# Causal attention: the next batch's part between values and scores, GpSimd's differences behind the parts, pauses around a transpose

## The chip, the cores and the metric

The kernel runs on one core of a Trainium2 chip. The metric is the device time of one execution in microseconds (us). TensorE (PE) multiplies matrices and transposes; its weight loads are shown as PEld. VectorE (DVE), ScalarE (ACT) and GpSimd (POOL) work on rows of 128 partitions; SyncE (SP) issues most transfers. Matrix products land in PSUM, of which the kernel uses eight banks, each 512 float32 wide, through one pool.

## The reference, cut to what matters

A network of four layers, each an attention and a mixture of experts, over 4 batches of 512 tokens of width 128, all in float32. Two of the four attentions are causal softmax attentions with 16 heads of width 8 for the values, and only these two run through the code that the change touches:

```python
# layer 0: scores with a bias by distance      # layer 1: scores as a product of two factors
att = einsum('bhtd,bhsd->bhts', q, k) / sqrt(D) + bias     logits = A1 * A2 * SCALE
att = softmax(where(causal, -inf, att))                    attn = softmax(where(causal, -inf, logits))
out = einsum('bhts,bhsd->bhtd', att, v) @ proj_w.T + b     out = einsum(attn, v) @ Wo.T + bo
```

Ahead of each attention a batch is normalized over its width (mean 0, variance 1). Layer 0's attention is followed by a top-1 routed mixture of experts whose routing is computed for each batch as soon as that batch's attention has ended.

## The kernel before, in words

**Units and steps.** `attention` (L566) works on 16 units: 4 batches b times 4 groups g of four heads. A unit has 4 steps j, one for each 128 queries; step j looks at the first (j+1)*128 keys. The work is a pipeline over units: while unit u is turned into weights and values, unit u+1 gets its scores. A step of the causal branch (L812 to L822) issues, in this order:

1. `weights(u, j)`: TensorE transposes the finished scores of unit u (1, 2, 4 and 4 PSUM banks for j = 0 to 3); ScalarE moves them to SBUF, with the exponential for two of the four heads.
2. `exponentials()`: ScalarE's exponentials for the other two heads of the scores made one step ago, kept in the list `put_off`.
3. `values_up_to`: TensorE multiplies the weights of the step before with the values.
4. `scores(u+1, j)`: four TensorE products into four banks; four DVE reductions (L604, L608) add bias or mask, find the largest of each row and write the scores `sc` to SBUF, which frees the banks; for two heads GpSimd then subtracts the largest (L605), right in this place of its queue.
5. the first slot, called "between" below (L821): one part of the next batch's beginning (`begin_next(u, True)`, not in units with u % 4 of 2 or 3), or else one part of a finished batch's routing (`go_on`).
6. at j = 0 `start(u+2)`, which forms the next unit's q and k (in layer 1 one product on DVE and one on GpSimd).
7. the second slot, called "tail" (L836 to L839): again a part of the next batch's beginning (not with u % 4 = 2), else of a routing.
8. on odd j a part of other work (`beside`: in layer 1 GpSimd's small copies and SP's loads of a later layer's weights), and at j = 2 and 3 the normalization and gathering of the unit before.

PE, DVE, ACT and POOL keep this order of the program in this region (`manual_schedule`); the queue of SP is put in order by a planner that uses its own costs. Where work of a later stage is placed among the attention's, that is the planner's too.

**The beginning of a batch** (`begin`, L968 for layer 0 and L1137 for layer 1) is a generator: each `yield` ends one part. Layer 0: (1) read and add the expert result; (2) statistics of tiles 0 and 1; (3) statistics of tiles 2 and 3 and GpSimd's reciprocal root (L157, L158); (4) DVE applies the norm to tiles 0 and 1 (L171); (5) to tiles 2 and 3; (6) `turned`: four TensorE transposes T (L180) into one bank and one copy nT by DVE or ACT (L127, L129, in turn); (7) q and k (L901 to L905); (8) values and the bias row (L857, L960). Layer 1 has no part (1), and its seventh place is three TensorE products "factors" (L1148), their copies, and nine transfers that write them to DRAM (L1155, L1159). Each unit of layer 1 later fetches its q and k factors from there with four transfers (L1176), issued three units ahead. Batch 0's parts all run ahead of the loop. For b = 1 the parts begin in unit 0; for b = 2 and 3 the first four run in the tails of units 3 and 7, and the rest in the slots of units 4 and 8.

**Routing** (`tokens`, L283) of a finished batch of layer 0 is a like generator of some 17 parts, from unit 4b+5 on, with its own norm, transposes, small products and, at its end, GpSimd's indirect transfers.

Of the kernel before, what the change touches and what calls it, by code (L numbers as in the profile page):

```python
# [11 lines left out]
AF = mybir.ActivationFunctionType  # L12
ALU = mybir.AluOpType
# [28 lines left out]
def kernel(ctx: ExitStack, tc: tile.TileContext, a: dict, out: bass.AP):  # L42
    nc = tc.nc
# [12 lines left out]
    def bank(name):  # L56
        return psum.tile([P, 512], FP, name=name, tag="bank", bufs=8)
# [66 lines left out]
    def copy(dst, src):  # L124
        n_copies[0] += 1
        if n_copies[0] % 2:
            nc.vector.tensor_copy(dst, src)  # L127
        else:
            nc.scalar.copy(dst, src)  # L129
# [46 lines left out]
    def transposed(src, tag):  # L176

        ps = bank(f"T_{tag}")
        for t in range(NT):
            nc.tensor.transpose(ps[:, t * P : (t + 1) * P], src[:, t, :], ident)  # L180
        return ps
# [6 lines left out]

    def turned(n, tag):

        nT = work.tile([P, S], FP, name=f"nT_{tag}", tag="nT", bufs=4)
        copy(nT, transposed(n, tag))
        yield
        return nT

# [370 lines left out]
    def attention(pool, tag, begin, project, residual, owT, added, after=None, beside=(), fetch=None):  # L566
# [8 lines left out]
        def begun(b):  # L575
            if ("begin", b) not in st:
                st["begin", b] = begin(b)
            return next(st["begin", b], "end") != "end"

        def start(u):  # L580
            b, g = units[u]
            if g == 0:
                st["o", b] = pool.tile([P, NT, NG, NG * HD], FP, name=f"otok_{tag}{b}", tag="otok")
            st["qk", u] = project(b, g)

        def product(ps, q, k, r, i, n0, n1):
            nc.tensor.matmul(  # L587
                ps[:, n0:n1], q[r : r + SLOT, i * P : (i + 1) * P], k[r : r + SLOT, n0:n1], start=True, stop=True
            )


        def scores(u, i):
            b, g = units[u]
            q, k = st["qk", u]
            n = (i + 1) * P
            banks = [bank(f"s_{tag}{u}_{i}{r}") for r in range(4)]
            for r in range(4):
                product(banks[r], q, k, r * SLOT, i, 0, n)
            for r in (2, 0, 3, 1):
                sc = pool.tile([P, n], FP, name=f"sc_{tag}{u}_{i}{r}", tag=f"sc{i}", bufs=4)  # L600
                top = small.tile([P, 1], FP, name=f"top_{tag}{u}_{i}{r}", tag="top", bufs=16)
                more = added(g * 4 + r)[:, S - n :]
                if r < 2:
                    nc.vector.tensor_tensor_reduce(sc, banks[r][:, :n], more, 1.0, -HUGE, ALU.add, ALU.max, top)  # L604
                    nc.gpsimd.tensor_scalar(sc, sc, top, None, ALU.subtract)  # L605
                else:

                    nc.vector.tensor_tensor_reduce(sc, banks[r][:, :n], more, -1.0, HUGE, ALU.add, ALU.min, top)  # L608
                    put_off.append((sc, top))
                st["sc", u, i, r] = sc  # L610

        put_off = []

        def exponentials():

            for sc, top in put_off:
                nc.scalar.activation(sc, sc, AF.Exp, bias=top, scale=-1.0)  # L617
            put_off.clear()

        def weights(u, i):  # L620
# [22 lines left out]
        def values_up_to(u, i):  # L643

            b, g = units[u]
            if i == 0:
                st["acc", u] = bank(f"acc_{tag}{u}")
            for j in range(i + 1):
                for r in range(4):
                    nc.tensor.matmul(  # L650
                        st["acc", u][r * SLOT : (r + 1) * SLOT, i * P : (i + 1) * P],
                        vpads[b % 2][:, j, g * 4 + r, :],
                        st["w", u, i, r][:, j * P : (j + 1) * P],
                        start=(j == 0),
                        stop=(j == i),
                    )
            if i == NT - 1:
                summed(u)
# [15 lines left out]
        def lowered(u):  # L674
            q, k = st["qk", u]
            ps = bank(f"low_{tag}{u}")
            for i in range(NT):
                nc.tensor.transpose(ps[:, i * P : (i + 1) * P], st["low", u][:, i, :], ident)  # L678
            ql = pool.tile([P, S], FP, name=f"ql_{tag}{u}", tag="ql", bufs=2)
            nc.vector.tensor_tensor(ql, ps, q, ALU.add)  # L680
            st["ql", u] = ql
# [20 lines left out]
        def together(*parts):  # L702

            live = [p for p in parts if p is not None]
            while live:
                for p in list(live):
                    made = next(p, None)
                    if made is None:
                        live.remove(p)
                    else:  # L710
                        made()
# [20 lines left out]
        def summed(u):  # L732
            o_u = pool.tile([P, S], FP, name=f"ou_{tag}{u}", tag="ou", bufs=3)
            nc.scalar.copy(o_u, st["acc", u])
            st["ou", u] = o_u
# [21 lines left out]
        rest = []  # L757
# [9 lines left out]
        def go_on():  # L767
            if rest and next(rest[0], "end") == "end":
                rest.pop(0)

        def begin_next(u, between=False):


            b = (u + 1) // NG + 1
            return u % NG not in ((2, 3) if between else (2,)) and b < NB and begun(b)
# [11 lines left out]
        with tc.manual_schedule(engines={E_.PE, E_.DVE, E_.Activation, E_.Pool}):  # L787
            while begun(0):
                pass
            for u in range(3):  # L790
                if fetch is not None:
                    fetch(*units[u])
                if u > 0:
                    start(u - 1)
            if added:
                for i in range(NT):
                    scores(0, i)
                    exponentials()
            else:

                for n in range(0, lead, 2):
                    if n == 2 * NT:
                        lowered(0)
                    together(step(largest, n), step(largest, n + 1))
            for u in range(n_units + 1):
                last = u - 1
                now, nxt = u < n_units, u + 1 < n_units
                for j in range(NT):
                    n = 2 * (u * NT + j)

                    of = (u, j - 1) if j > 0 and now else (last, NT - 1) if j == 0 and last >= 0 else None
                    if added:  # L812
                        if now:
                            weights(u, j)
                        exponentials()

                        if of:
                            values_up_to(*of)
                        if nxt:
                            scores(u + 1, j)  # L820
                        if rest or not begin_next(u, True):  # L821
                            go_on()  # L822
                    else:
                        together(step(largest, n + lead), step(by_key, n))
                        if of:
                            times_values(*of, 0)
                        if j == NT - 1 and nxt:
                            lowered(u + 1)
                        if rest or not begin_next(u, True):
                            go_on()  # L830
                        together(step(largest, n + 1 + lead), step(by_key, n + 1))
                        if of:
                            times_values(*of, 1)
                    if j == 0 and u + 2 < n_units:
                        start(u + 2)
                    if j == 0 and last >= 1 and units[last - 1][1] == NG - 1:  # L836
                        ended(units[last - 1][0])
                    elif not begin_next(u):
                        go_on()  # L839
                    if j % 2:  # L840
                        next(beside, None)
                    if j == 2 and last >= 0:
                        normalized(last)
                    if j == 3 and fetch is not None and u + 3 < n_units:
                        fetch(*units[u + 3])
                    if j == 3 and last >= 0 and units[last][1] == NG - 1:
                        gathered(units[last][0])
            ended(NB - 1)
            while rest:
                go_on()  # L850
# [275 lines left out]
    def l1_attn(beside):  # L1126
        with tc.tile_pool(name="attn1", bufs=2) as pool:
# [9 lines left out]
            def begin(b):  # L1137
                n = yield from normed(b, f"a1_{b}")
                nT = yield from turned(n, f"a1_{b}")


# [420 lines left out]
```

## Time and profile before

| | |
|---|---|
| median of 3 runs | 1575.8 us (1572.78 to 1575.96) |
| the profiled execution's own time | 1557.3 us |
| its span, first to last instruction | 1555.6 us |
| PE busy | 1279.9 us, 82% of the span |
| DVE, ACT, POOL busy | 866.6, 713.2, 657.2 us |
| mean granted TensorE clock | 0.898 |
| causal attention of layer 0 | from about 130 to 361 us |
| causal attention of layer 1 | from about 545 to 771 us |

Times inside the profile are microseconds from the start of the span. A line of the timeline gives start, duration, engine, line of the kernel, operation, what it writes and reads, shapes, how many like instructions are merged in it, and in brackets how long the engine had stood idle before it and what ended that. The list of waits gives, for an engine and a line, who released it, the sum in us, the number of times, and the longest. The profile is one execution; the runs of the first row are others.

### The profile page before, as it was taken

To read this page: it belongs to the slowest core of one execution; us is meant where nothing else is said; L and a number is where in the kernel's file an instruction comes from. 1 tells how busy PE (TensorE), PEld (TensorE's weight loads), DVE (VectorE), ACT (ScalarE), POOL (GpSimd) and SP (SyncE) were. 2 spreads that over 40 slices of the span, in tenths; PEclk is the share of its full clock that TensorE was granted. 3 is DMA by queue.
4 is the path that set the end of the run, shared out by engine and by line. 5 is a ranking of instruction groups with operands and counts; after the bars stand their busy time and mean duration, and the time that the engine had idled before them with its cause. 6 is when DMAs were issued, how large, how long until landed. Compare 5 with 4: busy or idle time off the path is not lost. (4 is left out here: it accounts for less than half of the span.)

```text
span 1555.6 us, 28883 instructions
## 1 busy us (share of the span) xinstructions
PE 1279.9 (82%) x10651; PEld 823.0 (53%) x10651; DVE 866.6 (56%) x2955; ACT 713.2 (46%) x1487; POOL 657.2 (42%) x791
## 2 busy tenths in 40 slices
PE   3787998995969688989989887819789999998394
PEld 3464666773755455757656666606533334333273
DVE  5325776773335366666556556615367787773343
ACT  1234876871443156768743322203336655564041
POOL 3455767772420177677510111263631224212253
PEclk9897999996989988999989878858979999999597
DMA  7520230002415375442022000014204000000233
GB/s 226 129 57 13 77 146 32 9 6 65 140 49 111 94 219 150 140 133 70 2 56 55 1 0 1 10 61 103 62 21 172 15 5 12 13 3 15 76 79 105
DMA packets 100660, 106.21 MB, mean 68 GB/s; under 512 B 9084, under 2 KB 73832, under 8 KB 100520
## 3 DMA queue, kind: packets, MB, share of 16 engines
q1 hardware_dynamic: 93864, 91.16, 20.8%
q0 software_dynamic: 6656, 13.22, 2.6%
q8 instruction: 84, 1.38, 0.4%
q14 instruction: 56, 0.46, 0.1%
HBM read 62.49 MB, written 41.85 MB: 67 GB/s over the span
## 5 line engine op out<-in xcount | busy, mean ns | idle before, releaser
L605 POOL TENSOR_SCALAR sc_a<-sc_a,top_a 128x128 f32<-128x128 f32 (+3 forms) x256 | 276.0, 1093 | 110.6 <-DVE top_a L604 75.1
L587 PE MATMUL s_a<-k_a,q_a 32*128 32x512 f32 (+3 forms) x1536 | 266.5, 548 | 17.1 <-POOL k_a L1183 13.8
L692 ACT ACTIVATE w_a<-t_a 128x512 f32<-128x512 f32 x256 | 140.4, 595 | 119.6 <-PE t_a L587 94.9
L628 PE MATMUL t_a<-ident,sc_a 128*128 128x128 f32 x1280 | 172.3, 282 | 6.2 <-DVE top_a L608 5.7
L489 POOL DMA_INDIRECT res_f<-y_f,back_f x112 | 109.8, 980 | 143.7 <-ACT y_f L488 102.3
L587 PE MATMUL t_a<-ql_a,k_a 32*128 32x512 f32 x512 | 168.8, 644 | 0.5 <-DVE low_a__12755 L672 0.2
L628 PEld LDWEIGHTS t_a<-ident,sc_a 128*128 128x128 f32 x1280 | 145.2, 144 | 36.4 <-issue 13.7
L617 ACT ACTIVATE sc_a<-sc_a,top_a 128x128 f32<-128x128 f32 (+3 forms) x256 | 134.9, 577 | 22.8 <-DVE top_a L608 22.6
L587 PEld LDWEIGHTS s_a<-k_a,q_a 32*128 32x128 f32 x1536 | 93.7, 188 | 88.1 <-issue 42.8
L637 ACT ACTIVATE w_a<-t_a 128x256 f32<-128x256 f32 (+2 forms) x192 | 94.3, 526 | 63.6 <-PE t_a L628 63.1
L395 POOL DMA_INDIRECT disp_f<-n_f,to_f x96 | 94.6, 985 | 66.7 <-issue 58.8
L501 PE MATMUL o_f<-w_l,h_f 128*128 128x128 f32 (+1 forms) x896 | 113.0, 279 | 3.8 <-DVE o_f L483 3.3
L501 PEld LDWEIGHTS o_f<-w_l,h_f 128*128 128x128 f32 (+1 forms) x896 | 103.0, 184 | 14.7 <-DVE o_f L483 6.0
L466 PE MATMUL h_f<-dT_f,w_l 128*128 128x320 f32 (+1 forms) x256 | 108.0, 560 | 2.8 <-ACT dT_f L444 2.8
L157 POOL TENSOR_SCALAR rs_f<-mv_f 128x4 f32<-128x4 f32 (+1 forms) x23 | 5.7, 248 | 230.0 <-DVE mv_f L154 229.2
L650 PE MATMUL acc_a<-w_a,vpad 128*32 128x128 f32 x2560 | 98.4, 280 | 0.6 <-DVE top_a L604 0.6
L639 ACT COPY w_a<-t_a 128x256 f32<-128x256 f32 (+2 forms) x192 | 93.7, 527 | 6.9 <-PE t_a L628 6.6
L672 DVE TENSOR_REDUCE low_a__12755<-s_a 128x1 f32<-128x512 f32 x128 | 82.1, 685 | 26.3 <-PE t_a L587 18.5
L608 DVE CUSTOM_DVE_ANT_0 sc_a<-s_a,future 128x128 f32<-128x128 f32 (+3 forms) x128 | 62.3, 487 | 56.4 <-PE s_a L587 50.3
L672 DVE TENSOR_REDUCE low_a__12753<-s_a 128x1 f32<-128x512 f32 x128 | 81.3, 683 | 20.1 <-PE t_a L587 15.0
L608 DVE CUSTOM_DVE_ANT_0 sc_a<-s_a,table 128x128 f32<-128x128 f32 (+3 forms) x128 | 62.4, 488 | 52.9 <-PE s_a L587 52.4
L488 ACT ACTIVATE y_f<-o_f,d_f 128x128 f32<-128x128 f32 (+1 forms) x112 | 38.8, 394 | 105.9 <-DVE o_f L483 105.9
(343 smaller groups left out, 2285.9 us busy)
## 6 DMA issues: line engine op xcount, KB each, us to landing
fac_a<-fac_a_sb SPq DMA_DIRECT2D x36, 256.0 KB
disp_f<-zeros_f SPq DMA_DIRECT2D x4, 2080.0 KB
d_f<-disp_f SPq DMA_DIRECT2D x32, 260.0 KB
w_l<-in_L_ffn_w_dram SPq DMA_DIRECT2D x16, 512.0 KB
cb_f<-rows_f SPq DMA_DIRECT2D x16, 512.0 KB
q_a<-fac_a SPq DMA_DIRECT2D x32, 256.0 KB
k_a<-fac_a SPq DMA_DIRECT2D x32, 256.0 KB
r_f<-res_f SPq DMA_DIRECT2D x24, 256.0 KB
```

Of the source, the lines that this page charges most:

```text
L395: nc.gpsimd.indirect_dma_start(out=self.to[c][i0 + t][:, :], out_offset=bass.IndirectOffsetOnAxis(ap=to[:, c, t : t + 1], axis=0), in_=ns[ ...
L466: nc.tensor.matmul(ps[u][:, :cap], w1[:, e, (c + u) * P : (c + u + 1) * P], dT, start=True, stop=True)
L489: nc.gpsimd.indirect_dma_start(out=self.back[e * per + s][:, :], out_offset=bass.IndirectOffsetOnAxis(ap=back[:m, s : s + 1], axis=0), in_ ...
L501: nc.tensor.matmul(po[:m, s, :], h[:, c, s * P : s * P + m], w2[:, e, c, :], start=(c == 0), stop=(c == NC - 1),)
L587: nc.tensor.matmul(ps[:, n0:n1], q[r : r + SLOT, i * P : (i + 1) * P], k[r : r + SLOT, n0:n1], start=True, stop=True)
L605: nc.gpsimd.tensor_scalar(sc, sc, top, None, ALU.subtract)
L608: nc.vector.tensor_tensor_reduce(sc, banks[r][:, :n], more, -1.0, HUGE, ALU.add, ALU.min, top)
L617: nc.scalar.activation(sc, sc, AF.Exp, bias=top, scale=-1.0)
L628: nc.tensor.transpose(ps[:, x * n + j * P : x * n + (j + 1) * P], st["sc", u, i, r0 + x][:, j * P : (j + 1) * P], ident,)
L650: nc.tensor.matmul(st["acc", u][r * SLOT : (r + 1) * SLOT, i * P : (i + 1) * P], vpads[b % 2][:, j, g * 4 + r, :], st["w", u, i, r][:, j * ...
L672: nc.vector.tensor_reduce(st["low", u][:, i, c : c + 1], ps, AX.X, ALU.max, negate=True)
L692: nc.scalar.activation(w, ps, AF.Exp)
```

## The change

Three edits, all of them in the order in which instructions are issued; the number and the shapes of the instructions stay the same.

- In `turned`, one empty part is put ahead of the transposes and one behind the copy, so that a beginning has ten parts in layer 0 and nine in layer 1. In an empty part nothing is issued.
- GpSimd's differences go into the list `put_off` together with ScalarE's exponentials and are issued by `exponentials()`, which is called one step later, behind `weights` (and right behind `scores` for the first unit). In GpSimd's queue they so stand behind the parts of both slots of their step.
- The first slot is moved from behind `scores` to ahead of them.

```diff
     def turned(n, tag):
 
+        yield
         nT = work.tile([P, S], FP, name=f"nT_{tag}", tag="nT", bufs=4)
         copy(nT, transposed(n, tag))
+        yield
         yield
         return nT
...
                 if r < 2:
                     nc.vector.tensor_tensor_reduce(sc, banks[r][:, :n], more, 1.0, -HUGE, ALU.add, ALU.max, top)
-                    nc.gpsimd.tensor_scalar(sc, sc, top, None, ALU.subtract)
+                    put_off.append((sc, top, True))
                 else:
                     nc.vector.tensor_tensor_reduce(sc, banks[r][:, :n], more, -1.0, HUGE, ALU.add, ALU.min, top)
-                    put_off.append((sc, top))
+                    put_off.append((sc, top, False))
...
         def exponentials():
-            for sc, top in put_off:
-                nc.scalar.activation(sc, sc, AF.Exp, bias=top, scale=-1.0)
+            for sc, top, less in put_off:
+                if less:
+                    nc.gpsimd.tensor_scalar(sc, sc, top, None, ALU.subtract)
+                else:
+                    nc.scalar.activation(sc, sc, AF.Exp, bias=top, scale=-1.0)
             put_off.clear()
...
                         if of:
                             values_up_to(*of)
+                        if rest or not begin_next(u, True):
+                            go_on()
                         if nxt:
                             scores(u + 1, j)
-                        if rest or not begin_next(u, True):
-                            go_on()
```

## The prediction

> **What bounds the kernel now.** I first read the windows view of two undisturbed units of layer 0's attention, for each engine's busy time.
>
> ```profile
> core 0: us, PE busy (x) PEld busy (x) DVE busy (x) ACT busy (x) POOL busy (x), PEclk, DMA share, GB/s
> 162.56:174.07 11.51, 11.50 (x160) 7.96 (x157) 7.30 (x34) 10.02 (x23) 8.04 (x9) 1.00 0.01 2
> 174.07:185.58 11.51, 11.50 (x161) 7.97 (x157) 8.84 (x39) 10.02 (x23) 9.02 (x10) 1.00 0.82 254
> ```
>
> A unit is 11.51 us and TensorE is busy for 11.50 of them at full clock. A plain unit can't get shorter by a reordering; only the idle time at the parts of a next batch can go. The list of waits from 130 to 361 us says who ends that idle time:
>
> ```profile
> POOL sc_a L605 <- DVE top_a L604: 51.5, 25, 7.0
> PE T_a L180 <- DVE n_a L171: 11.6, 6, 3.4
> ```
>
> TensorE stands 11.6 us before the transposes T in six waits, two for each of batches 1, 2 and 3. GpSimd stands 51.5 us in its differences, with everything behind them in its queue, the norm's root among it. The timeline shows the chain for batch 1:
>
> ```profile
> 141.90 0.23 POOL L157 TENSOR_SCALAR rs_a<-mv_a 128x4 f32<-128x4 f32 x1
> 142.21 1.04 POOL L158 TENSOR_TENSOR rstd_a<-rs_a,mhalf 128x4 f32<-128x4 f32 x1
> 143.28 0.60 DVE L171 TENSOR_SCALAR n_a<-x,mv_a,rstd_a 128x128 f32<-128x128 f32 x2 [2.57 <-POOL rstd_a L158]
> 143.68 0.59 PE L180 MATMUL T_a<-ident,n_a 128*128 128x128 f32 x2 [2.79 <-DVE n_a L171]
> 146.40 0.69 PE L180 MATMUL T_a<-ident,n_a 128*128 128x128 f32 x2 [2.13 <-DVE n_a L171]
> 146.88 3.62 PE L628 MATMUL t_a<-ident,sc_a 128*128 128x128 f32 x16
> ...
> 174.56 1.91 PE L628 MATMUL t_a<-ident,sc_a 128*128 128x128 f32 x16
> ```
>
> The root comes at 141.90 because twelve differences (11.89 us from 130.03) are ahead of it. DVE applies half of the norm, then the four reductions of a score stand before the other half. TensorE, in order, waits for both. The last two lines show a second price: sixteen transposes took 3.62 us after the wait and 1.91 us in a plain unit.
>
> ```profile
> 145.00:151.80 6.80, 5.40 (x42) 4.70 (x42) 1.41 (x6) 3.58 (x7) 2.50 (x2) 0.50 0.00 0
> 250.80:257.60 6.80, 5.19 (x29) 3.46 (x30) 2.76 (x13) 2.36 (x5) 4.18 (x4) 0.50 0.00 0
> 619.40:622.80 3.40, 3.00 (x4) 1.45 (x5) 0.94 (x2) 0.59 (x1) 3.23 (x4) 0.50 0.02 5
> ```
>
> The granted clock was 0.50 behind three of the waits. Layer 1 has the same chain and two more things:
>
> ```profile
> 563.40 1.27 PE L180 MATMUL T_a<-ident,n_a 128*128 128x128 f32 x4 [3.67 <-DVE n_a L171]
> 593.68 0.69 DVE L1183 TENSOR_TENSOR q_a<-q_a,q_a 128x512 f32<-128x512 f32 x1 [4.80 <-DMA q_a<-fac_a]
> 619.80 2.08 PE L1148 MATMUL fac_a<-nT_a,qk1T 128*128 128x512 f32 x2 [1.07 <-DVE nT_a L127]
> 565.00:595.00 30.00, 25.17 (x294) 17.12 (x295) 15.10 (x65) 18.65 (x41) 18.47 (x23) 0.90 0.98 298
> ```
>
> The factors' products wait for the copy nT made just before them, and the first batch of layer 1 is handed over through a DMA that was busy for 0.98 of 30 us.
>
> **What the Trainium skill says.** "TensorE: Matmul & The Clock Gate", Part 1, says the clock falls to half when the array has idled for a window of about 3.4 us and is given back after a busy one; the trace agrees as to length (stretches of 6.8 and 3.4 us at 0.50). The same page, under "Architectural detail", calls the queues of ACT, DVE and GpSimd strict FIFO; here that is the root behind twelve differences. "PSUM — Partial Sum Buffer", Specifications, gives eight banks: a step with four banks of scores, up to four of transposes and one accumulator is already at that number, so late reductions can hold TensorE up. The trace shows this at 608.84: 0.44 us before a transpose, ended by a reduction, after 1.9 us of other DVE work.
>
> **The change part by part, layer 0.** No instruction is added. Counting slots gives the new places.
>
> *Batch 1.* Before, the second half of the norm was in step 2's first slot and T in its second. After: norm halves in step 1's tail and ahead of step 2's scores, an empty part, T ahead of step 3's scores. The root has ten differences ahead of it instead of twelve; the two of width 256 took 1.83 us, so it ends near 141.5 instead of 143.25. DVE then applies all four tiles by 143.0, while TensorE, free since 140.9, has 16 transposes and 24 value products to do until about 145. Saved: 2.79 + 2.13 = 4.92 of waiting. With the wait the slow clock goes: transposes 3.62 - 1.91 = 1.71, values (the row at 150.43 against that at 176.40) 1.50 - 0.86 = 0.64. Sum 7.3.
>
> *Batch 2.* Waits 1.44 and 1.07. Now the second half is ahead of step 0's reductions (free at 192.5, done at 194.0), and T follows step 1's transposes and values, near 193.6. Left: about 0.4. Saved 2.1.
>
> *Batch 3.* Waits 3.41 and 0.80; the root started at 249.35 behind differences of width 384 (2.48 us). After, it stands ahead of these, done near 248.2, when DVE is still at its reductions (until 248.8). Second half done at 250.4, T due at 249.7: left 0.6. Slow clock saved: step 1's transposes 1.91 - 1.04, scores 1.24 - 0.71, values 0.66 - 0.42, together 1.64 (the partners are batch 2's). Saved 3.6 + 1.6 = 5.2. **Layer 0: 14.6 us.**
>
> The q and k products (2 us) move ahead of a score, values and bias row by two slots; their first use is four steps or more later, so nothing. The differences (1.19, 1.83, 2.47, 3.11 us for two) are needed three steps later at the soonest; POOL's 164 busy us of 231 in this window cover the delay. Passed by them are the root, k's product (1.27), the bias row (1.28), L533's copies and the indirect transfers (0.96 to 1.13 each); these only come earlier.
>
> **New waits.** A first slot's DVE work now stands ahead of four reductions. For routing, the root is in a tail and its use in the next first slot, with nothing between: the root needs 0.23 + 1.04 plus some 0.3 of passing on, then 0.75 of applying. Reductions come about 2.2 us later than before; TensorE has W(3), 3 banks and ScalarE's releases to go on with. By the 0.44 above I charge 0.5 for each of three routings: **-1.5**; from below 0, from above the whole 2.2 each.
>
> **Layer 1.** *Batch 1* has one part fewer, so the root is in step 0's tail and the first half now ahead of step 1's reductions. POOL still works off the first unit's eight differences and k until 560.4, so the root ends at 561.75 (before 562.80), and the reductions of step 1 wait until 562.5 with four banks held. TensorE then stops in step 2's scores near 559.7 and resumes near 563: the old 3.67 in another place. The factors come a step later (out near 572 instead of 568). SP's queue gets the nine writes later, but the weight loads, released by L533's copies, go out about 1.5 us earlier, and the four fetches follow both. The saturated DMA sets the landing at 593.68 either way: from the earlier start -1.7, from writes that come late and must land before the fetches +3.5. I take 0 for this hand-over.
> *Batches 2 and 3*: T keeps its place behind step 0's scores, and its 0.88 us stays; the factors move a step on, and 1.07 goes twice: 2.1. Batch 2's slow stretch (factors to next transpose 4.17 us, batch 3 2.68) would be another 1.5; a wait near the limit may cross it again, so I take 0 and keep it for the range. **Layer 1: 2.1.**
>
> Sum: 14.6 - 1.5 + 2.1 = 15.2, say **15 us**. The profiled execution's own 1557.3 would become about 1542. The median of the runs, 1575.8, is 18.5 us above that execution; a difference of 1% needs no scaling, so I forecast **1561**. Unpriced: the planner may reorder SP and the early norm of the next stage at 692 to 700 (2.4 us of waiting and a slow stretch today), 3 us either way.
>
> **Rivals.**
> - *Half.* The waits at T go, but TensorE stops at full banks a little later, as in layer 1's batch 1. For: 608.84. Against: in layer 0 two of the three first halves stay in a tail. Clock losses then stay: 14.6 less 4, less 2.2 x 3 for routing, plus 2.1, about 6: 1570.
> - *Nothing.* The time won is waited for at a transfer. For: the 4.80 us at 593.68. Against: layer 0's end leads to no transfer that is already under way. 1575.
> - *Slower.* DVE waits for the root in front of four reductions, in three routings and layer 1's first batch: 2.2 us each become a full stop of TensorE, followed by a slow stretch of the size above (2.35): 4 x 4.6 = 18, and the late fetch 3.5, together 21.5 against 16.7 won: 1580. It decides if TensorE's stock of banks covers less than about 1.5 us of DVE's delay; 608.84 says that some 1.9 cost 0.44, against it.
> - That the order is not what the diff says: the four engines follow the program here, so hardly.
>
> **How the numbers follow.** Forecast 0.66, half 0.15, nothing 0.06, slower 0.13. About 0.2%, 3 us, is what a measurement can tell from no change: the first two are faster, 0.81; within it 0.06; slower 0.13. Forecast alone 1555 to 1569 (DMA -1.7, clock -1.5, planner -3; bounds of routing 5, planner 3 the other way). To leave out no more than 2 in 10: 1553 to 1575.
>
> **What would show it.** Right: the wait of TensorE for n falls from 11.6 to under 2 us in layer 0, no 0.50 clock near 145 and 250, L605's idle time down. Wrong: new idle time before L628 or L587 ended by L604 or L608, DVE waiting for L158 in the routing's norms, or a longer wait at 593.

## The result and the profile after

| | before | changed |
|---|---|---|
| median of 6 runs each | 1573.99 us | 1555.24 us |
| lowest to highest | 1572.36 to 1575.96 | 1552.4 to 1557.95 |
| ratio, with its 95% interval | | 0.988 (0.9863 to 0.9896) |
| the profiled execution's own time, span | 1557.3, 1555.6 | 1552.8, 1550.8 |
| mean granted TensorE clock | 0.898 | 0.903 |

The change won 18.9 us; 15 were forecast. The two profiled executions differ by only 4.5 us. That need not contradict the 18.9, because by all signs they come from different chips. One chip ran the kernel before in 1573 us, two others ran it in 1556 and 1557 (medians). The profile that the forecast was made from, 1557.3, lies outside the range of the first (1565.65 to 1580.34) and inside those of the others. The traces say the same: one unit of the last layer's attention takes 21.13 to 21.32 us in every profile from the slower chip, and 21.25 in the profile after; it takes 15.96 to 15.97 in every profile from the two quick chips, and 15.98 in the profile of before. So below, "before" is compared with a profile of the changed kernel from one of the quick chips, called all_again, and the first profile after, from the slower chip, is set beside a profile of before from that same chip (before_again).

The busy line and the group of GpSimd's differences, from the page of the kernel after (the group has busy time, mean ns of one, and idle time ahead of it with its main releaser):

```profile
PE 1279.1 (82%) x10651; PEld 820.5 (53%) x10651; DVE 867.0 (56%) x2955; ACT 713.3 (46%) x1487; POOL 656.8 (42%) x791
L621 POOL TENSOR_SCALAR sc_a<-sc_a,top_a 128x128 f32<-128x128 f32 (+3 forms) x256 | 274.9, 1089 | 91.4 <-DVE top_a L606 57.0
```

Counts and work are as they were; only idle time, and time lost to the slow clock, can have gone. GpSimd now stands 91.4 us ahead of its differences (110.6 before). The list of waits of the kernel after from 130 to 361 us (sum, number, longest):

```profile
POOL sc_a L621 <- DVE top_a L606: 26.4, 15, 2.9
PE t_a L634 <- DVE top_a L610: 6.3, 8, 1.9
DVE n_f L171 <- POOL rstd_f L158: 5.9, 4, 1.5
```

GpSimd's 51.5 us at its differences have become 26.4, and TensorE's line for T and the norm, 11.6 us before, is no longer in the list. In its place are two lines that the prediction named as signs of harm: transposes that wait for reductions, 6.3 us in eight waits, and DVE waiting for the root in the routing's norm (`n_f`), four times 1.5. The longest of the eight, 1.9 us, is missing in all_again, where the line has 4.4 us in seven waits. The timeline for batch 1, after:

```profile
137.44 1.04 POOL L158 TENSOR_TENSOR rstd_a<-rs_a,mhalf 128x4 f32<-128x4 f32 x1
138.51 1.45 DVE L171 TENSOR_SCALAR n_a<-x,mv_a,rstd_a 128x128 f32<-128x128 f32 x4 [0.52 <-POOL rstd_a L158]
141.87 0.66 PE L180 MATMUL T_a<-ident,n_a 128*128 128x128 f32 x4
```

The four tiles of the norm are applied in one go, 1.9 us ahead of T, and T runs as one group without a stop. The windows of the kernel after at the two places of layer 0 where the clock had been 0.50, and as third line the window of all_again around layer 1's first hand-over (us, busy time of PE, PEld, DVE, ACT, POOL, granted clock, DMA share, GB/s):

```profile
140.00:147.00 7.00, 6.73 (x83) 3.65 (x80) 5.11 (x17) 5.49 (x11) 4.62 (x5) 1.00 0.01 2
240.00:248.00 8.00, 7.85 (x67) 4.56 (x65) 4.70 (x23) 6.63 (x15) 8.00 (x8) 1.00 0.00 1
550.00:580.00 30.00, 28.05 (x332) 19.57 (x333) 17.67 (x74) 20.81 (x45) 21.09 (x20) 0.96 0.99 307
```

The slow stretches of layer 0 are gone. The hand-over's window begins about when the weight loads do, as the prediction's window of before did. The DMA is as full in it as before (0.99, before 0.98), but TensorE is busy for 28.05 of its 30 us instead of 25.17, at a granted clock of 0.96 instead of 0.90.

### The profile page after: what moved, and what is told of

The parts are those of the page before. It is cut to its first block, busy times and chain, and to the rows that moved or that the text cites. A ratio compares the mean times of both kernels' runs of the same rounds, so it can differ in the third digit from the quotient of the medians.

```text
span 1550.8 us, 28862 instructions
## 1 busy us (share of the span) xinstructions
PE 1279.1 (82%) x10651; PEld 820.5 (53%) x10651; DVE 867.0 (56%) x2955; ACT 713.3 (46%) x1487; POOL 656.8 (42%) x791
## 3 DMA queue, kind: packets, MB, share of 16 engines
q0 software_dynamic: 6656, 13.22, 2.6%
## 5 line engine op out<-in xcount | busy, mean ns | idle before, releaser
L621 POOL TENSOR_SCALAR sc_a<-sc_a,top_a 128x128 f32<-128x128 f32 (+3 forms) x256 | 274.9, 1089 | 91.4 <-DVE top_a L606 57.0
L678 DVE TENSOR_REDUCE low_a__12753<-s_a 128x1 f32<-128x512 f32 x128 | 81.4, 683 | 24.8 <-PE t_a L589 16.3
```

Source lines behind the costliest of these rows:

```text
L678: nc.vector.tensor_reduce(st["low", u][:, i, c : c + 1], ps, AX.X, ALU.max, negate=True)
```

## The experiments

The theory of the prediction: the time won lies in the beginnings of batches 1 to 3, and part of it is paid back in the routings, whose DVE work now stands ahead of four reductions. Rivals: the win belongs to the pauses alone; or it comes from transfers in layer 1. All ratios are to the kernel before on the same chip, with their 95% intervals. The first four kernels ran on the slower chip, the others on the quick ones.

**Before, unchanged.**

> The kernel before, unchanged, for a second profiled execution. The profiled execution on record took 1557.3 us, the timed ones 1572 to 1576; the stage sums of the two profiles differ by 4.5 us only, the timed medians by 18.7. Theory (the gain is in the two causal attentions and the profile of before was a lucky one elsewhere): this profile is near 1574, and the 17 us more lie outside the causal attentions, in stretches at a clock of 0.5. Rival (the lucky part is in the attentions themselves): the 17 us more lie between 130 and 361 or 545 and 771 us. Ratio 1.000.

Measured: 1.000 (0.9987 to 1.0012), 1573.88 us; its profile has a span of 1571.9, 16.3 us more than the profile of before. Neither theory nor rival holds alone: 6.2 us of that lie in layer 0's attention, layer 1's is 1.0 us shorter, and the rest lies outside both.

**One edit at a time**: pauses; diffs; slot.

```diff
 # pauses
+        yield
         nT = work.tile([P, S], FP, name=f"nT_{tag}", tag="nT", bufs=4)
         copy(nT, transposed(n, tag))
+        yield
         yield
 # diffs
-                    nc.gpsimd.tensor_scalar(sc, sc, top, None, ALU.subtract)
+                    put_off.append((sc, top, True))
 # slot
+                        if rest or not begin_next(u, True):
+                            go_on()
                         if nxt:
                             scores(u + 1, j)
-                        if rest or not begin_next(u, True):
-                            go_on()
```

> Only the two empty parts in turned; slots and differences stay. Theory of the waits at T: in layer 0 the transposes come one slot later, behind a finished norm, so nearly all of 11.6 us of waiting and some 4 us of slow clock go; in layer 1 the factors' waits (1.07 twice) go and T's 3.67 stays; no routing part is moved, so nothing is lost there: -15 to -20 us, ratio 0.987 to 0.990. Rival (the waits go only when all three edits are there, since the root is behind the differences): -5 us, ratio 0.997.

> Only GpSimd's differences are put off behind the parts. Theory: the root comes 1.1 to 2.5 us sooner, T's first waits of batches 1 and 3 shrink by that much, the second halves still stand behind four reductions: -4 us, ratio 0.9975. Rival (late differences hold up DVE or TensorE, because the buffers of the largest values come free later): no gain or +3 us, ratio 1.002.

> Only the first slot is moved ahead of the scores. Theory: T's second waits in layer 0 (2.13, 1.07, 0.80) go, the first waits stay in part, and the routing's norms stand ahead of the reductions, which in the changed kernel's profile made seven units of layer 0 longer by 0.1 to 2.3 us, 9.5 in all: +3 us, ratio 1.002. Rival (the longer units come from the put-off differences, not from the slot): -5 us, ratio 0.997.

Measured: pauses 0.9895 (0.9877 to 0.9914), as expected; diffs 0.9941 (0.992 to 0.9961), more than twice the gain expected; slot 0.999 (0.9978 to 1.0003), no difference that can be told, where a loss was expected. So the pauses carry most, but not all. By stages, against before_again (239.21 us for layer 0's attention, 244.18 for layer 1's): pauses takes 12.7 us from layer 0's attention and 4.1 from layer 1's, diffs 4.8 and 0.7, and slot takes 5.7 from layer 0's and adds 3.0 to layer 1's. The expectation for slot had missed that, alone, it too brings a beginning's DVE work forward (TensorE's wait at T for batches 1 to 3 of layer 0 falls from 10.3 to 5.4 us). The rest of what diffs won lies in stages that it does not touch and is not explained.

**Two edits, and all three again.**

```diff
 # pauses_diffs, pauses_diffs_2: the first two edits above
 # pauses_slot: the first and the third
 # all_again: the three, as in the change
```

> Pauses and put-off differences; the first slot stays behind the scores. Theory (the slot edit costs layer 0 the 5 us that its routing loses in front of the reductions, and brings layer 1 a hand-over without a wait for a transfer): layer 0's attention near 226 us as with the pauses alone (229 with all three edits), layer 1's near 239, the time about that of all three edits, ratio 0.987 to 0.989. Rival (the slot edit is what makes the last 3 us): ratio 0.9895 to 0.991, as with pauses alone.

> Pauses and put-off differences a second time, to stand beside all three edits on one chip: ratio 0.9845, 5 us less than all three edits. Rival: no difference.

> Pauses and the first slot ahead of the scores; the differences stay in their place. Theory: the slot puts the use of the root ahead of the reductions while GpSimd's differences are still ahead of the root, so the routing's loss is at its largest: layer 0's attention about 231 us or more, ratio 0.990 to 0.993, worse than pauses alone (0.9895). Rival (pauses make the slot's place indifferent): 0.9895.

> All three edits, on the same chip as the next three. Theory (the pauses and the put-off differences carry the gain, the slot edit gives some of it back in layer 0): ratio to before 0.988 as measured at first, so slower than pauses with put-off differences by 0.3%. Rival (the ratios differ by chip alone): 0.9845 on a chip on which those two edits give 0.9845.

Measured: pauses_diffs 0.9846 (0.9826 to 0.9866), the same kernel on another chip 0.9846 (0.9832 to 0.9859), pauses_slot 0.9941 (0.9928 to 0.9955), all_again 0.9865 (0.9849 to 0.988). The first two edits add up (1.05% and 0.59% against 1.54% together). The third takes away from the first: pauses_slot has a higher ratio than pauses alone, by intervals that do not meet (each to its own chip's kernel before). On top of both, the third moves the median from 1532.84 to 1535.45 on one chip, with intervals that overlap. For pauses_diffs 0.987 to 0.989 was expected, with layer 0's attention near 226 us; it came out lower, with 218.82. For pauses_diffs_2 a median 5 us below all_again's was expected; it is 2.6 us below. For pauses_slot 0.990 to 0.993 was expected, so it lost a little more, while its layer 0 took 230.80 us, about as expected (231): the norm's root is still behind the differences there, TensorE waits 2.11 us at T of batch 3, and unit 8 takes 20.88 us. The 0.988 expected for all_again lies at the edge of its interval.

What diffs does beside the pauses is seen at batch 3 of layer 0. The timeline of the kernel pauses_held (below; in layer 0 it is pauses alone):

```profile
238.97 2.48 POOL L607 TENSOR_SCALAR sc_a<-sc_a,top_a 128x384 f32<-128x384 f32 x2
241.43 0.22 POOL L157 TENSOR_SCALAR rs_a<-mv_a 128x4 f32<-128x4 f32 x1
241.74 1.04 POOL L158 TENSOR_TENSOR rstd_a<-rs_a,mhalf 128x4 f32<-128x4 f32 x1
242.82 0.99 DVE L171 TENSOR_SCALAR n_a<-x,mv_a,rstd_a 128x128 f32<-128x128 f32 x2 [1.85 <-POOL rstd_a L158]
244.07 1.12 PE L589 MATMUL s_a<-k_a,q_a 32*128 32x256 f32 x8 [2.41 <-DVE top_a L610]
```

With the differences in their old place the root still waits for two of width 384; DVE stands 1.85 us at the norm, the reductions come behind it, and TensorE stops 2.41 us in its scores. The pause alone had moved the stop from T to the scores. Unit 8 takes 18.85 us here, 14.91 with diffs too, 21.14 before. How much this costs varies from execution to execution: in the profile of pauses, from the slower chip, the root stands behind the same two differences, but DVE waits only 0.51 us for it, TensorE stops 1.07 us, and unit 8 takes 15.90 us.

**Only the routing's part back behind the scores**: all three edits, but where a routing is under way its part stays in the old place. This is the direct test of the cost of the routings.

```diff
-                        if rest or not begin_next(u, True):
-                            go_on()
+                        if not rest:
+                            begin_next(u, True)
+                            began = True
+                        else:
+                            began = False
                         if nxt:
                             scores(u + 1, j)
+                        if not began:
+                            go_on()
```

> All three edits, but only the next batch's parts go ahead of the scores; a routing's part in the first slot stays behind them. Theory (routing parts on DVE, with a wait for the root of 1.46 us or a string of small operations, stand in front of four reductions and so hold PSUM banks): the waits of TensorE for a reduction, 0.5 to 0.9 us twice per routing, go, units 5, 6, 9, 10, 13 and 14 are back at their former length, -5 us against all three edits, ratio 0.9845. Rival (those waits come from the put-off differences): ratio 0.988 as with all three.

Measured: 0.9844 (0.9826 to 0.9862). From its list of waits, 127 to 350 us:

```profile
DVE n_f L171 <- POOL rstd_f L158: 1.5, 1, 1.5
```

The line of transposes that wait for reductions is no longer in the list, and DVE's wait for the root in a routing is left once (batch 3's, behind the last unit). Layer 0's attention is 221.54 us, against 224.93 for all_again. The interval of the ratio overlaps all_again's, so it is the traces that show the cost of the routings here, and not the times.

**The later layer's weight loads held back**: with the pauses, and with pauses and diffs, the loads that `beside` issues in layer 1 start two units later. It tests whether the fetches of the hand-over are late because they share the DMA with these loads.

```diff
+        def held(parts):
+            for _ in range(4):
+                yield
+            yield from parts
-        l1_attn(lambda pool: prep_l3_ffn(xs[0]))
+        l1_attn(lambda pool: held(prep_l3_ffn(xs[0])))
```

> Pauses alone, and in layer 1 the loads of the later layer's weights (4 MB) start two units later, so that they do not share the DMA with the first hand-over's nine writes and four fetches. Theory (the 3.24 us before a transpose at 583 us with pauses alone is this sharing): that wait goes and with it a slow stretch, unit 18 falls from 16.2 to about 12 us, -4 to -5 us against pauses alone, ratio 0.9865. Rival (the fetch is late by its own chain of write and read): ratio 0.9895 and the wait stays.

> Pauses, put-off differences and the later weight loads. Theory: adds to the former what the differences bring in layer 1 (T's 3.66 us shrinks to about 2.4): ratio 0.985 to 0.9865, below all three edits. Rival (the pauses take everything that the differences could bring): the same as pauses with later loads.

Measured: 0.9883 (0.9863 to 0.9903) and 0.9847 (0.9827 to 0.9866): no difference that can be told from pauses and pauses_diffs. Yet the stop that was aimed at is gone. In pauses TensorE stopped 3.24 us at 582.7 at the hand-over of batch 1 and unit 18 took 16.21 us; with the loads held back it takes 11.22 (11.21 in pauses_diffs_held). The loads are then in the way of the next hand-over, and unit 20 takes 22.36 us instead of 16.45. The timeline of pauses_held there:

```profile
601.52 0.69 DVE L1185 TENSOR_TENSOR q_a<-q_a,q_a 128x512 f32<-128x512 f32 x1 [3.96 <-DMA q_a<-fac_a]
602.12 0.68 DVE L127 COPY nT_a<-T_a 128x512 f32<-128x512 f32 x1
602.96 1.10 PE L1150 MATMUL fac_a<-nT_a,qk1T 128*128 128x512 f32 x2 [3.94 <-DVE nT_a L127]
```

DVE stands 3.96 us at a product whose factors are late, with the copy nT behind it in its queue, and TensorE 3.94 us at the factors of batch 2, which need nT. The stop was moved, not removed.

**The first slot ahead of the scores in layer 1 only**, with pauses and diffs everywhere.

```diff
-                        if rest or not begin_next(u, True):
+                        early = after is None
+                        if early and (rest or not begin_next(u, True)):
                             go_on()
                         if nxt:
                             scores(u + 1, j)
+                        if not early and (rest or not begin_next(u, True)):
+                            go_on()
```

> Pauses and put-off differences everywhere, the first slot ahead of the scores in layer 1 alone, where no routing runs. Theory: layer 0 as with pauses and put-off differences (218.8 us), layer 1 as with all three edits and routing behind (234.5 against 237.4, since all weight loads then go ahead of the hand-over's writes): 2 to 3 us less than pauses with put-off differences, ratio 0.9825 to 0.983, below every kernel so far. Rival (the hand-over's order is the planner's accident and turns out otherwise): 0.9845.

Measured: 0.9836 (0.9822 to 0.9849), 1531.63 us, the lowest ratio of all. All its runs (up to 1532.72) lie below those of all_again on the same chip (from 1533.83), so it beats the changed kernel. Its interval overlaps that of pauses_diffs_2, so it is not shown to beat the first two edits alone. The traces give it 219.59 us for layer 0's attention, as expected, and 236.64 for layer 1's, where 234.5 was expected.

## Why the prediction was right, and where its terms were off

Lengths of stages and units, from the traces (a unit ends where ScalarE begins to copy its last values out of PSUM; all four columns are taken to be from quick chips), in us:

| | before | all_again | pauses_diffs | routing_behind |
|---|---|---|---|---|
| layer 0's attention | 232.98 | 224.93 | 218.82 | 221.54 |
| of it unit 4 (batch 2 begins) | 17.12 | 16.04 | 15.38 | 16.03 |
| unit 8 (batch 3 begins) | 21.14 | 15.75 | 14.91 | 15.72 |
| units 9 and 10 (a routing) | 13.59, 13.08 | 14.75, 13.74 | 13.59, 13.22 | 13.59, 13.23 |
| layer 1's attention, from its first factors | 245.22 | 236.55 | 237.35 | 234.54 |
| of it unit 18 (batch 1 handed over) | 17.84 | 13.48 | 17.12 | 13.14 |
| unit 20 (batch 2 handed over) | 19.22 | 16.60 | 16.44 | 16.59 |

Against the prediction's terms, before to all_again:

| term | predicted | measured |
|---|---|---|
| layer 0, batch 1 (units 0 and 1) | -7.3 | -6.7 |
| layer 0, batch 2 | -2.1 | -1.1 |
| layer 0, batch 3 | -5.2 | -5.4 |
| three routings (nine units) | +1.5 | +5.1 |
| layer 1, hand-over of batch 1 (units 16 to 18) | 0 | -5.0 |
| layer 1, batches 2 and 3 (units 20 and 24) | -2.1 | -3.8 |
| sum | -15.2 | -16.9 |

The two stage lengths of layer 0 and layer 1 together give 16.7; the rest of the measured gain is taken up under "smaller terms". The pair from the slower chip, before_again and after, gives the same picture: -13.3 for the three beginnings of layer 0, +3.4 for the routings, -3.7 for the hand-over and -4.0 for units 20 and 24.

That the total came so near is in part luck. The routings lost 3.6 us more than was charged and the hand-over won 5.0 that were not counted, and these two errors largely cancel.

**The beginnings in layer 0 were right**, in mechanism and size: 13.1 us won of 14.6 forecast, waits and slow clock both. (Ahead of the three slow stretches that the prediction shows, TensorE had not been idle all the time: it was busy for 0.59, 0.81 and 1.85 of the 3.4 us.) The first table also shows what the prediction did not separate: the first two edits alone do this (units 4 and 8 are shorter still without the third).

**The routing's term failed by size.** The prediction took 0.44 us as the measure of a late reduction and charged 0.5 once for each routing. (Its count of banks was short by one: four, four and one are nine, more than the eight that the kernel has.) A routing has two such places. The first is the one named; the timeline of the kernel after, batch 0's routing:

```profile
204.87 1.04 POOL L158 TENSOR_TENSOR rstd_f<-rs_f,mhalf 128x4 f32<-128x4 f32 x1
205.95 0.60 DVE L171 TENSOR_SCALAR n_f<-x,mv_f,rstd_f 128x128 f32<-128x128 f32 x2 [1.46 <-POOL rstd_f L158]
206.46 0.55 DVE L610 CUSTOM_DVE_ANT_0 sc_a<-s_a,table 128x384 f32<-128x384 f32 x1
207.08 0.81 PE L634 MATMUL t_a<-ident,sc_a 128*128 128x128 f32 x5 [0.74 <-DVE top_a L610]
```

DVE waits for the root, applies half of the norm, and only then reduces; TensorE stops 0.74 us before its transposes (in all_again's three routings 0.73, 0.91 and 0.92). The second place was not counted at all:

```profile
219.90 0.77 DVE L361 TENSOR_TENSOR pre_f<-pre_f,masks_f 128x8 f32<-128x8 f32 x4
220.62 0.56 DVE L610 CUSTOM_DVE_ANT_0 sc_a<-s_a,table 128x384 f32<-128x384 f32 x1
221.24 1.14 PE L634 MATMUL t_a<-ident,sc_a 128*128 128x128 f32 x8 [0.47 <-DVE top_a L610]
```

Small routing operations of DVE, the last of which is the first line here, fill 218.04 to 220.62 ahead of the reductions, and TensorE stops 0.47 us (0.47, 0.54 and 0.54 in all_again's three). The six stops of all_again are 4.1 of the 5.1 us; routing_behind takes them away and brings units 9, 10, 13 and 14 back to within 0.15 us of before. (Its unit 6 is long instead, 15.54 us against 14.04 before; that one unit varied from 14.0 to 15.6 us over the kernels, and why is open.) This also bounds the rival Slower: the mechanism is real, but a stop is 0.5 to 0.9 us and not 2.2, and no slow clock follows (the granted clock in the 4 us behind each of the six stops is 1.00 in all_again). The 0.44 us at 608.84, which the prediction held against this rival, was the right kind of evidence, but the stops of the first place are twice as long.

**The hand-over in layer 1 was missed.** Taken as 0 between -1.7 and +3.5, it was -5.0. TensorE's first stop did move from T to step 2's scores as described (after: 2.95 us, before at T: 3.67):

```profile
553.71 0.66 DVE L171 TENSOR_SCALAR n_a<-x,mv_a,rstd_a 128x128 f32<-128x128 f32 x2 [3.66 <-POOL rstd_a L158]
554.76 1.56 PE L589 MATMUL s_a<-k_a,q_a 32*128 32x384 f32 x4 [2.95 <-DVE top_a L610]
```

What the prediction missed begins with the order of SP's queue, which the planner makes. Before (start, duration of the issue, line, what is written):

```profile
567.17 0.58 SPq L538 DMA_DIRECT2D w_l<-in_L_ffn_w_dram  x1
568.18 0.34 SPq L1155 DMA_DIRECT2D fac_a<-fac_a_sb  x1
569.40 7.47 SPq L1159 DMA_DIRECT2D fac_a<-fac_a_sb  x8
576.93 0.65 SPq L539 DMA_DIRECT2D w_l<-in_L_ffn_w_dram  x1
...
583.40 3.35 SPq L1176 DMA_DIRECT2D q_a<-fac_a  x2
```

and after:

```profile
565.81 0.47 SPq L541 DMA_DIRECT2D w_l<-in_L_ffn_w_dram  x1
566.38 2.44 SPq L1161 DMA_DIRECT2D fac_a<-fac_a_sb  x1
568.91 7.08 SPq L1165 DMA_DIRECT2D fac_a<-fac_a_sb  x8
576.18 2.20 SPq L1182 DMA_DIRECT2D q_a<-fac_a  x2
582.19 0.69 DVE L1189 TENSOR_TENSOR q_a<-q_a,q_a 128x512 f32<-128x512 f32 x1 [0.64 <-DMA q_a<-fac_a]
```

Before, five of the eight weight loads stood between the factors' writes and the fetches; the fetch issued at 583.40 had its data used at 593.68, after a wait of 4.80 us. After, all eight stand ahead of the writes, the fetch goes out at 576.18, and the product waits 0.64 us at 582.19. The prediction held that the saturated DMA sets the landing either way. The DMA is as full as before, yet the time from the fetch's issue to the use of its data fell from 10.3 to 6.0 us.

Of the 5.0 us, 4.4 lie in unit 18. The order alone does not explain them. In the table, issue and use are counted in us from the end of unit 16, the stop is TensorE's wait for a reduction in unit 18 (none means none over 0.4 us), and the clock is the granted one from there, or without a stop from the use of the data, to the end of the unit.

| | loads ahead of the first write | fetch issued | data used | stop | clock | unit 18 |
|---|---|---|---|---|---|---|
| before | 3 of 8 | 6.8 | 17.1 | 4.48 | 0.82 | 17.84 |
| before_again | 3 of 8 | 4.9 | 15.1 | 2.48 | 0.84 | 15.55 |
| pauses_diffs | 8 of 8 | 10.1 | 16.2 | 2.66 | 0.74 | 17.12 |
| pauses_diffs_2 | 8 of 8 | 12.2 | 18.1 | 4.53 | 0.82 | 17.83 |
| all_again | 8 of 8 | 9.4 | 15.6 | 1.95 | 1.00 | 13.48 |
| after | 8 of 8 | 8.0 | 14.0 | none | 1.00 | 11.84 |
| slot_layer1 | 8 of 8 | 7.7 | 13.9 | none | 1.00 | 11.69 |
| pauses_held | none | 4.8 | 13.1 | none | 1.00 | 11.22 |

In both profiles of pauses and diffs all eight loads stand ahead of the writes too, and the fetch takes only some 6 us; but it is issued so late that the data come about as late as before. With the third edit in layer 1 it goes out earlier. So the order alone did not shorten unit 18; it became short where the loads stood ahead of the writes and the fetch went out earlier too. The gain has two parts: the stop falls from 4.48 to 1.95 us in all_again, and the slow clock that followed every stop of 2.48 us or more in this table did not follow that of 1.95. Why the fetch goes out earlier with the third edit was not tested. In these traces the weight loads start 10.2 to 11.8 us ahead of the end of unit 16 with all three edits in layer 1, 7.6 and 9.3 in the two without the third; that this is the reason is argued only.

Without the loads at this place (pauses_held) there is no stop, so they are needed for it. Whether they act by their share of the DMA or by their turn in SP's queue, these runs do not separate. That the order is the planner's is how the kernel is built; why it chose it was not tried.

**Smaller terms.** T's 0.88 us in layer 1 stays twice, as said. Batch 2's slow stretch there, kept for the range at 1.5, did go: unit 20 won 2.6, batch 3's unit 24 the predicted 1.1. The stop of 2.40 us in the scores ahead of the next stage (at 698.69 before) stays at 675.49 in all_again, so the planner's unpriced 3 us did not come there. Outside the two attentions all_again is shorter by another 5.9 us (1.9 ahead of layer 0's, 4.5 between the two). Among kernels that don't differ there these stretches ran from 118.2 to 121.6 and from 169.8 to 174.9 us, with the profile of before at the top of both, so none of it is put down to the change; why they differ stays open.

**The offset.** "18.5 us between execution and median" was taken for scatter between executions of one kernel; by the signs given above it was the difference between two chips. The forecast came through it unharmed because it added a difference in us to the median.

## What to carry to other kernels

Before a part is moved ahead of work that frees a shared buffer, list everything that goes through the same slot, not only the part that is meant: here, once the pauses and the put-off differences were in, layer 0's beginnings gained nothing from the move, and the routings that shared the slot lost 4 to 5 us by it. A pause between two dependent steps helps less if the step it waits for is queued behind unrelated work: with the root still behind the differences, the stop in batch 3 only moved from T to the scores. Where a planner orders a DMA queue, read the order of its issues again after any change of other engines' order, and read beside it when the transfer that is waited for goes out: with the same order of loads and writes unit 18 took 17.83 us in one kernel and 11.69 in another.

## What the runs showed of the hardware that was not expected

The same kernel ran in 1573 us on one chip and in 1556 and 1557 on two others, 1% apart and steady on each. The profiles of before put 7.4 us of that in two units of the last layer's attention, which none of these kernels changes: 21.29 against 15.98 and 13.70 against 11.63 us. Another 6.2 us lie in layer 0's attention, in units with the routing's indirect transfers among others; there, on the slower chip, one stop of 1.89 us at 293.64 in the profile after has no counterpart in all_again. Why that chip differs was not found.
